# Ten batches of seven and eight key blocks a group in place of twelve of six, with the steps around them laid out anew

## The chip, the cores and the metric

The kernel runs on one core of a Trainium2 chip. The metric is the device time of one execution in microseconds (us). Engines are named as in the profile: PE (TensorE, matmuls), PEld (its weight loads), DVE (VectorE), ACT (ScalarE), POOL (GpSimd) and SP (SyncE, which here only issues DMAs).

## The reference

The input is a batch of four images of 384 channels and 48 x 48 = 2304 tokens, in float32. For each image:

- a depthwise 7 x 7 convolution with batch norm, then a layer norm over the channels: `local_q`;
- a layer norm of the image's tokens, then projections to queries, keys and values of eight heads of 48 channels;
- `q = q + local_q`, and attention of all 2304 tokens to all 2304 tokens in each head: `softmax(q k^T / sqrt(48)) v`;
- an output projection, a bias, and the image itself added.

```python
q = q + local_q
attn = jax.nn.softmax(jnp.einsum('bhnd,bhmd->bhnm', q, k) * scale, axis=-1)
out = jnp.einsum('bhnm,bhmd->bhnd', attn, v)
...
out = x_flat + (out @ proj_w.T + proj_b)
```

## The kernel before

**Tiling.** An image's queries are cut into five groups (8, 10, 10, 10 and 10 rows of 48 tokens, so 384 or 480 columns), which makes groups t = 0 to 19 over the four images; g = t mod 5. Heads are taken in four pairs p. The keys are 18 blocks of 128 tokens. So a group is 4 x 18 = 72 blocks, each a pair of heads against 128 keys.

**A block.** `score` (line 1105) multiplies the keys, in a high and a low part, with the queries, in a high and a low part: three steps, each a pair of matmuls on the two halves of the array's rows, into a PSUM buffer `r`. ScalarE takes the exponential into a tile `pt` (line 1113), of which there are four. `weigh` (line 1120) multiplies the values with `pt`, one head in each half of the array's columns, into a buffer `o`; the value's extra column of ones gives the softmax's denominator. All PSUM buffers, `r`, `o` and those of the projections, come from one pool of four, each of two banks, in turn.

**A batch.** `score_batch` issues the scores of six blocks, `weigh_batch` then weighs the six. A group has twelve such slots s, three to a pair of heads. ScalarE copies each batch's sum out of PSUM: the first of a pair to the output `ao` (line 1007; for the fourth pair to `aot`), the second and third to a tile `part_o` (line 997, two buffers), and VectorE adds it to the first in the next slot (`sums_add`, line 1016). After the last add of a pair SyncE stores the denominators (`den`, line 1021), and after the fourth pair it moves pieces of `aot` into `ao` (the tails, line 1025).

**Work between.** All engine queues are written out by hand, in the order of the loop over slots. VectorE's largest work is the convolution of later groups (line 340), one instruction a tap, handed out by `convolve` at two points in each slot; `plan` computes how many from an estimate of VectorE's spare time (`spare`) and from when each group's convolution is due. Around it stand:

- the next query: a norm in steps (`Norm`: sum, centre, squares on ScalarE at line 561, sum of squares, variance, root, then `local_end` and `query_end`). For groups up to 4 the means are matmuls (line 593), and VectorE waits for the root at line 631; later groups send partial sums through DRAM (`out`, then `few_in` at line 656);
- the norm of the next image's tokens, by the same steps, in an image's last groups;
- the split of each pair's queries: `high_queries` (a cast on ScalarE, line 968), `low_queries` (a subtraction on VectorE at line 973, then six DMAs on SyncE, lines 978 and 980). Pairs 1 to 3 are split in the first slot of the pair before. The fourth pair's queries are first gathered from the others' tails into `qt` (`gather_tails`, line 700, eight DMAs on SyncE), at s = 0;
- the previous group's division (`divide`, at s = 2): SyncE reads the denominators into `rd` (line 1032), VectorE takes reciprocals (line 1042), and SyncE spreads them; the product is taken at s = 7 (line 1446) and stored by POOL;
- the keys: a third of a pair's keys (six blocks, tile `ks`, three buffers) is loaded two slots ahead (`load_keys`, line 766), by POOL, and by ScalarE's queue at the start of an image.

Between images, keys and values of the next image are projected (line 694), with the output projection of the image before.

Of the kernel before, what the change touches and what calls it, by code (L numbers as in the profile page):

```python
# [25 lines left out]
BATCH = 6  # L26
NSLOT = 12
X_SLOTS = 4, 7
X_LATER = 3
OUT_SLOT = 7  # L30
# [18 lines left out]
def unshifted_pass(  # L49
# [120 lines left out]
    third = BATCH * P  # L170
# [257 lines left out]
    def norm_slots(t):  # L428
        return (8 - (t > 0), None) if t + 1 < NA else (5, 8)

    def spare(t, s, half):
        b, g = divmod(t, NA)
        first, second = norm_slots(t)
        time = 3.6 - (0.0 if half else 0.6) - (0.6 if half and s % 3 == 1 else 0.0)
        if b + 1 < B and g >= begins(b + 1):
            time -= {(2, 1): 2.3, (4, 1): 2.2, (5, 1): 2.3, (7, 0): 0.4, (8, 0): 2.6}.get(
                (s, half), 0.0
            )
        if g:
            time -= {(2, 0): 0.7, (7, 1): 1.4}.get((s, half), 0.0)  # L440
        if t + 1 < NA:
            if t:
                time -= {
                    (first, 0): 1.3,
                    (first + 1, 0): 1.4,
                    (first + 1, 1): 1.3,
                    (first + 2, 1): 4.3,
                    (first + 3, 1): 0.6,
                }.get((s, half), 0.0)
            else:  # L450
                time -= {(first + 1, 0): 1.4, (first + 2, 0): 4.3, (first + 2, 1): 0.6}.get(
                    (s, half), 0.0
                )
        elif g < NA - 1:
            time -= {
                (3, 1): 2.3, (5, 0): 1.2, (5, 1): 2.2, (6, 1): 2.3, (8, 0): 0.4, (8, 1): 1.5,
                (9, 0): 4.5,
            }.get((s, half), 0.0)
        return max(0.3, time) * columns_of(t) / G
# [21 lines left out]
    for t in range(NT):  # L481
        if t % NA == 0 and t:
            points += [("kv", t, g, h) for g in range(NG) for h in range(5)]
            room += [spare_at_keys(t // NA, g, h) for g in range(NG) for h in range(5)]
        points += [("slot", t, s, h) for s in range(NSLOT) for h in range(2)]
        room += [spare(t, s, h) for s in range(NSLOT) for h in range(2)]
# [4 lines left out]
    for t in range(1, NT):  # L491
        last = ("slot", t - 1, norm_slots(t - 1)[0] - (t >= NA), t < NA) if t % NA else ("kv", t, 4, 0)
# [203 lines left out]
    def gather_tails(dst, src):  # L696

        for i, c in enumerate((*range(CC), 0)):
            for r in (0, 64):
                nc.sync.dma_start(  # L700
                    out=dst[r + 16 * i : r + 16 * i + 16], in_=src[r + HD : r + 64, c, :]
                )
# [65 lines left out]
    def from_x(b, g, before=None, ao=None):  # L768
# [22 lines left out]
        def key(u, r):  # L791
# [7 lines left out]
            else:  # L799
                k = work.tile([P, 2, GM], HALF, tag="pt", name=f"k{b}_{g}_{u}", bufs=4)[:, :, :G]  # L800
# [143 lines left out]
    def query_end(t, at_once=False):  # L944
# [3 lines left out]
        q3 = work.tile([P, GM], F32, tag="qt", name=f"qt{t}", bufs=1)[:, : columns_of(t)]  # L948
        queries[t] = q, q3
# [36 lines left out]
    ended = []  # L986
    parts_of = deque()

    def sums_out():

        if not ended:
            return
        t, p, i, sums = ended.pop()
        n = columns_of(t)
        if i:
            part = work.tile([P, GM], F32, tag="part_o", name=f"o{t}_{p}_{i}")[:, :n]
            nc.scalar.copy(part[0 : 64 + HA], sums[0 : 64 + HA, 0, :n])  # L997
            parts_of.append((t, p, i, part))
            return
        if p == 0:  # L1000
            ao = work.tile([P, CC, GM], F32, tag="ao", name=f"ao{t}")[:, :, :n]
            ao3 = work.tile([P, GM], F32, tag="aot", name=f"aot{t}", bufs=1)[:, :n]
            den = dram.tile([NH, n], F32, tag=f"den{n}", name=f"den{t}")
            outputs[t] = ao, ao3, den
        ao, ao3, den = outputs[t]
        dst = ao[:, p, :] if p < CC else ao3
        nc.scalar.copy(dst[0 : 64 + HA], sums[0 : 64 + HA, 0, :n])  # L1007

    def sums_add():
# [3 lines left out]
        t, p, i, part = parts_of.popleft()  # L1013
        ao, ao3, den = outputs[t]
        dst = (ao[:, p, :] if p < CC else ao3)[0 : 64 + HA]
        nc.vector.tensor_add(dst, dst, part[0 : 64 + HA])  # L1016
        if i < KB // BATCH - 1:
            return
# [3 lines left out]
        if p == NP - 1:  # L1022
            for c in range(CC):
# [71 lines left out]
    jobs, between = deque(), deque()  # L1095
    weighing = deque()

    def score(t, p, kb):
        ks, qs = stacks[t // NA, p, kb // BATCH], stacked[t, p]
        at = slice(kb % BATCH * P, (kb % BATCH + 1) * P)  # L1100
# [11 lines left out]
        pt = work.tile([P, 2, GM], F32, tag="pt", name="pt", bufs=4)[:, :, :n]  # L1112
# [3 lines left out]
    def weigh(i, sums):  # L1116
        t, p, kb, pt = weighing.popleft()
        for j in range(2):
            first = (kb % NB * NH + 2 * p + j) * HA
            nc.tensor.matmul(  # L1120
                sums[halves[j], 0, : columns_of(t)],
                lhsT=values[t // NA, kb // NB][:, first : first + 64],
                rhs=pt[:, j, :],
                start=i == 0,
                stop=i == BATCH - 1,
            )

    def score_batch(t, s):
        p, k0 = s // (KB // BATCH), s % (KB // BATCH) * BATCH
        for kb in range(k0, k0 + BATCH):  # L1130
            score(t, p, kb)
            if between:
                between.popleft()()

    def weigh_batch(t, s):
        p, i = s // (KB // BATCH), s % (KB // BATCH)
# [4 lines left out]
        sums = two_banks("o")  # L1141
        for n in range(BATCH):
            weigh(n, sums)
        ended.append((t, p, i, sums))
        sums_out()
# [139 lines left out]

    for t in range(NT):
        b, g = divmod(t, NA)
        if g == 0 and b:

            sums_add()  # L1290
            load_x(b, NG - 1)
# [68 lines left out]
        first, second = norm_slots(t)  # L1360
        for s in range(NSLOT):
            pair, part = divmod(s, KB // BATCH)
            score_batch(t, s)
            if part == 0 and pair < NP - 1:
                high_queries(t, pair + 1)
            if s == 0:
                gather_tails(*reversed(queries[t]))
            if s == 0 and g == 0:
                keep_stack(b, 2)
            if (s or g) and (s < NSLOT - 2 or g < NA - 1):  # L1370
                load_keys(b, s + 2, nc.scalar if g == 0 and s < 3 else nc.gpsimd)
            if s == 2 and g:
                rb = divide(t - 1)
            if s == 0 and coming:
                load_x(b + 1, g - begins(b + 1))
            if s == NSLOT - 4 and g == NA - 1:
# [4 lines left out]
                else:  # L1381
                    places = [("acc", 3)] * 3 + [("sq", 2)] * 2 + [("qs", 5)]
                    aos = []
                    for i in range(NG):
                        load_residual(b, i, *places[i])
                        aos.append(fetch(b, i) if i < NG - 1 else outputs[t][0])
            if coming and s == X_SLOTS[1] + 1:
                norm_x.scale(norm_x.few_newton())
            if following and s == second + 1:
                local_end(t + 1, norm.few_newton())  # L1390
                query_end(t + 1, True)
            if coming and s == X_SLOTS[0] + 1:
                jobs.extend(norm_x.square_jobs())
            if following and s == first + 1:
                jobs.extend(norm.square_jobs())
            if coming and s == X_SLOTS[1]:
                norm_x.few_variance()
            if following and s == second:
                norm.few_variance()
# [3 lines left out]
            else:  # L1403
                convolve("slot", t, s, 0)
            sums_add()
# [8 lines left out]
            if coming and s == X_SLOTS[1]:  # L1414
                norm_x.few_root()
            if following and s == second:
                norm.few_root()
# [3 lines left out]
            weigh_batch(t, s)  # L1421
            if early and s == first:
# [5 lines left out]
            if early and s == first + (2 if t == 0 else 3):  # L1428
                low_queries(t + 1, 0)
            convolve("slot", t, s, 1)  # L1430
            if t and early and s == first + 2:
                local_end(t + 1, norm.newton())
                query_end(t + 1)
            if part == 0 and pair < NP - 1:
                low_queries(t, pair + 1)
            if t and early and s == first + 1:
                norm.sum_squares()
            if following and s == second + 1:
                low_queries(t + 1, 0)
            if coming and s == X_SLOTS[0]:  # L1440
                norm_x.few_centre()
            if following and s == first:
                norm.few_centre()
            if s == OUT_SLOT and g:
                ao = outputs[t - 1][0]
                nc.vector.tensor_mul(ao, ao, rb)
                hold(t - 1)
            if coming and s == X_SLOTS[0] - 2:
                norm_x = Norm(xn[b + 1, g - begins(b + 1)])
                norm_x.sum()  # L1450
                norm_x.out()
            if coming and s == X_SLOTS[0] + 1:
                norm_x.sum_squares()
                norm_x.out()
            if following and s == first - 2:
                norm = Norm(accs[t + 1])
                norm.sum()
                norm.out()
            if following and s == first + 1:
                norm.sum_squares()  # L1460
                norm.out()

    sums_add()
    for i, at in enumerate(pieces_out):
# [556 lines left out]
```

## Time and profile before

| | |
|---|---|
| Runs, us | 2743.88, 2743.94, 2736.79; median 2743.88 |
| The profiled execution's own time, us | 2739.04 |
| Its span, us | 2737.2 |
| Granted TensorE clock | 0.997 |
| PE / DVE / ACT busy, share of the span | 99% / 85% / 61% |
| Chain that ended last: PE o L1120, PE r L1105, PE r L694 | 42%, 34%, 13% |
| Score matmuls L1105, number and mean | 8640, 373 ns |
| Weighing matmuls L1120, number and mean | 5760, 554 ns |
| Exponentials L1113, number and mean | 1440, 943 ns |

A line of the timeline has start, duration, engine, line, operation, what it writes and reads with shapes, and how many instructions are merged in it; in brackets stands the idle time of the engine before it and what ended that. SPq is SyncE's queue of DMA issues. Matmuls overlap their neighbours, so the time of a run is read from its start to the start of the next, not from means. A weighing counts as two records in each half[...].

### The profile page before, as it was taken

Reading aid. Unit: us, or ns where it says so; the run is one execution under the profiler, and the core shown is the slowest. Engines: PE = TensorE matmul, PEld = TensorE weight load, DVE = VectorE, ACT = ScalarE, POOL = GpSimd, SP = SyncE. Lnnn points to the kernel's source line nnn. Section 1 sums busy time; section 2 is a strip of 40 time slices with the busy share of each in tenths; the row PEclk is TensorE's granted clock in tenths of the full one; section 3 lists DMA queues with packets and bytes.
Section 4 is the critical chain, followed back from the end, with each engine's and each line's share of the span. In section 5 each row is a group of like instructions: output and inputs, shape, how many; then the busy total and the mean of one; then the engine's idle time right before and its main releaser. Section 6 shows DMA issues by size and latency. Waiting matters only on the chain.

```text
span 2737.2 us, 46047 instructions
## 1 busy us (share of the span) xinstructions
PE 2714.7 (99%) x16438; PEld 1536.6 (56%) x16438; DVE 2314.8 (85%) x4038; ACT 1671.1 (61%) x2317; POOL 603.9 (22%) x1077
## 2 busy tenths in 40 slices
PE   8999999999999999999999999999999999999999
PEld 5565555555556555555555655555555565555555
DVE  7999999989999999989889999889888998986212
ACT  4356777777325777777622677777752377776762
POOL 5541101102453111011155211111225511110110
PEclk9999999999999999999999999999999999999999
DMA  8354544446465545354555553545635544444442
GB/s 164 85 143 136 142 115 129 124 136 182 101 160 154 139 120 146 115 152 124 143 140 138 166 147 110 142 126 141 152 105 158 147 140 133 139 132 132 139 150 68
DMA packets 160223, 370.46 MB, mean 135 GB/s; under 512 B 58672, under 2 KB 107472, under 8 KB 159984
## 3 DMA queue, kind: packets, MB, share of 16 engines
q0 software_dynamic: 71424, 279.04, 35.6%
q1 hardware_dynamic: 83248, 78.33, 12.6%
q10 hardware_dynamic: 5312, 10.06, 1.1%
q8 instruction: 132, 2.16, 0.3%
q14 instruction: 107, 0.88, 0.1%
HBM read 258.14 MB, written 64.14 MB: 118 GB/s over the span
## 4 chain that ended last, share of the span: by engine, by line
PE 90%; DVE 5%; DMA 4%; ACT 0%; issue 0%; SPq 0%; POOL 0%; DVEq 0%; POOLq 0%; ACTq 0%
PE o L1120 42%; PE r L1105 34%; PE r L694 13%; DVE acc L340 2%; DMA parts<-part 1%; DMA staged<-in_qkv_wT_dram 1%; DVE k L804 0%; DMA slab<-in_x_dram 0%; PE r L415 0%; DMA four<-parts 0%; DVE xn L689 0%; DMA wide<-k 0%; DMA xn<-in_x_dram 0%; DMA out_dram<-xr 0%; DVE xr L1086 0%
## 5 line engine op out<-in xcount | busy, mean ns | idle before, releaser
L340 DVE SCALAR_TENSOR_TENSOR acc<-slab,vec,acc 128x470 f32<-128x470 f32 (+10 forms) x2832 | 1658.1, 658 | 2.0 <-ACT acc L303 2.0
L1113 ACT ACTIVATE pt<-r 128x960 f32<-128x960 f32 (+1 forms) x1440 | 1248.6, 943 | 246.4 <-PE o L1120 151.8
L1120 PE MATMUL o<-pt,v 128*64 128x480 f32 (+1 forms) x5760 | 1166.2, 554 | 0.4 <-ACT pt L1113 0.4
L1105 PE MATMUL r<-qs,ks 64*128 64x480 f32 (+1 forms) x8640 | 967.0, 373 | 4.8 <-ACT xn L818 3.0
L1105 PEld LDWEIGHTS r<-qs,ks 64*128 64x128 f32 x8640 | 785.2, 184 | 268.2 <-issue 171.6
L1120 PEld LDWEIGHTS o<-pt,v 128*64 128x64 f32 x5760 | 392.5, 137 | 659.9 <-issue 566.5
L766 POOL DMA_DIRECT2D ks<-wide x220 | 160.0, 727 | 1369.7 <-PE r L1105 1310.0
L694 PE MATMUL r<-xn,w_qk 128*128 128x384 f32 x864 | 284.7, 487 | 0.0
L997 ACT COPY o<-o 113x480 f32<-113x480 f32 (+1 forms) x160 | 87.1, 544 | 277.3 <-PE o L1120 276.7
L694 PEld LDWEIGHTS r<-xn,w_qk 128*128 128x128 f32 x864 | 164.4, 191 | 115.3 <-issue 1.8
L694 PE MATMUL r<-w_v,xn 128*128 128x384 f32 x432 | 145.3, 489 | 2.8 <-DVE xn L689 1.4
L788 ACT COPY v<-r 128x384 f32<-128x384 f32 x72 | 32.0, 479 | 183.3 <-PE r L694 183.3
L1016 DVE TENSOR_TENSOR ao<-ao,o 113x480 f32<-113x480 f32 (+1 forms) x120 | 75.9, 633 | 73.9 <-ACT o L997 73.9
L694 PEld LDWEIGHTS r<-w_v,xn 128*128 128x128 f32 x432 | 81.1, 190 | 62.6 <-DVE xn L689 3.8
L973 DVE TENSOR_TENSOR qs<-xn,qs 128x480 fp32r<-128x480 f32 (+1 forms) x60 | 38.1, 635 | 63.8 <-ACT qs L968 63.8
L751 POOL DMA_DIRECT2D wide<-k x144 | 72.4, 505 | 78.3 <-ACT k L801 64.2
L694 PE MATMUL r<-af,w_o 128*128 128x384 f32 (+1 forms) x270 | 85.2, 470 | 0.0
L1007 ACT COPY ao<-o 113x480 f32<-113x480 f32 (+1 forms) x60 | 32.6, 544 | 72.1 <-PE o L1120 72.1
L1016 DVE TENSOR_TENSOR aot<-aot,o 113x480 f32<-113x480 f32 (+1 forms) x40 | 25.4, 634 | 56.9 <-ACT o L997 56.9
L818 ACT ACTIVATE xn<-r,qkb 128x384 f32<-128x384 f32 x72 | 39.6, 576 | 50.8 <-PE r L694 47.6
L1086 DVE SCALAR_TENSOR_TENSOR xr<-r,pb,xr 128x384 f32<-128x384 f32 (+2 forms) x72 | 42.0, 611 | 33.2 <-PE r L694 26.0
L694 PEld LDWEIGHTS r<-af,w_o 128*128 128x128 f32 x270 | 51.3, 190 | 31.9
(148 smaller groups left out, 1354.9 us busy)
## 6 DMA issues: line engine op xcount, KB each, us to landing
ks<-wide POOLq DMA_DIRECT2D x220, 768.0 KB, 4.9
qs<-qs SPq DMA_DIRECT2D x352, 60.0 KB
slab<-in_x_dram POOLq DMA_DIRECT2D x24, 432.0 KB, 7.2
wide<-k POOLq DMA_DIRECT2D x96, 96.0 KB, 2.2
wide<-ks POOLq DMA_DIRECT2D x12, 768.0 KB, 5.3
xr<-in_x_dram POOLq DMA_DIRECT2D x16, 576.0 KB, 5.6
rb<-rden SPq DMA_DIRECT2D x32, 270.0 KB
held<-ao POOLq DMA_DIRECT2D x12, 720.0 KB, 3.9
```

The lines of the kernel that those rows point to most:

```text
L340: nc.vector.scalar_tensor_tensor(dst, src, weight, dst, ALU.mult, ALU.add)
L694: nc.tensor.matmul(dst, lhsT=weights(c), rhs=src(c), start=c == 0, stop=c == CC - 1)
L751: nc.gpsimd.dma_start(out=last[16 * u : 16 * u + 16, 0], in_=k[r : r + 16, 0])
L766: queue.dma_start(out=place_keys(b, p, i), in_=wide[b, p][:, :, at])
L818: nc.scalar.activation(src[:, i, :], q[:, :G], AF.Identity, bias=qkb[:, 0, i : i + 1])
L973: nc.vector.tensor_sub(qs[:, 1, :], query_of(t, p), qs[:, 0, :])
L997: nc.scalar.copy(part[0 : 64 + HA], sums[0 : 64 + HA, 0, :n])
L1016: nc.vector.tensor_add(dst, dst, part[0 : 64 + HA])
L1086: nc.vector.scalar_tensor_tensor(xr[:, co, :], m, pb[:, co : co + 1], xr[:, co, :], ALU.add, ALU.add)
L1105: nc.tensor.matmul(r[:, j, :n], lhsT=ks[rows, w, at], rhs=qs[rows, m, :], start=i == 0, stop=i == 2,)
L1113: nc.scalar.activation(pt, r[:, :, :n], AF.Exp, scale=SCALE)
L1120: nc.tensor.matmul(sums[halves[j], 0, : columns_of(t)], lhsT=values[t // NA, kb // NB][:, first : first + 64], rhs=pt[:, j, :], start=i == ...
```

## The change

Groups 4 to 19 (`few_slots`: t + 1 >= 5) get ten slots of 7, 7, 7, 7, 8, 7, 7, 7, 7 and 8 blocks; groups 0 to 3 keep twelve of six. Slots 2 and 7 of ten hold the end of one pair and the start of the next (`crosses`): the weighing then fills two buffers `o`, each copied out by itself, and the pending add is taken ahead of the slot's convolution. So a group still has 12 copied sums and 8 adds.

Buffers: `pt` has five tiles instead of four; `part_o` has one instead of two; `aot` loses its own tile and takes the single buffer of `qt`. For that, `tails_out` (the six copies of tails) and `gather_tails` become steps of their own, in this order: in slot 0 ahead of the weighing in groups of twelve slots, in slot 2 in groups of ten.

The norm steps, the division and the product are placed by two tables, PLACES_12 and PLACES_10, as (slot, stage), where stage 0 is ahead of the slot's first convolution, 1 ahead of the weighing, 2 after it and 3 after the second convolution. PLACES_12 keeps the places of before, but for tails. In groups of ten, centring and squares stand in the same slot and stage, the division's reciprocal at (1, 1), the product at (5, 1), the high split of pairs 1 to 3 in slots 0, 2 and 4, and the first high split of the next group's queries between exponentials (`in_gap`). The plan's estimates and due times follow the slots. Key loads are issued after the slot in which a third ends, all by POOL in groups of ten.

```diff
+THIRD = 6
+PLACES_12 = {
+    "x_sum": (2, 3), "x_centre": (4, 3), "x_squares": (5, 0), "x_sum_squares": (5, 3),
+    "x_variance": (7, 0), "x_root": (7, 1), "x_scale": (8, 0),
+    "divide": (2, 0), "tails": (0, 1), "multiply": (7, 3), "fetch": (8, 0),
+}
+PLACES_10 = {
+    "x_sum": (1, 3), "x_centre": (3, 1), "x_squares": (3, 1), "x_sum_squares": (3, 3),
+    "x_variance": (5, 1), "x_root": (5, 1), "x_scale": (5, 3),
+    "divide": (1, 1), "tails": (2, 1), "multiply": (5, 1), "fetch": (7, 0),
+    "q_sum": (2, 3), "q_centre": (4, 1), "q_squares": (4, 1), "q_sum_squares": (4, 3),
+    "q_variance": (6, 1), "q_root": (6, 1), "q_end": (6, 3), "q_high": (6, 3), "q_low": (7, 3),
+}
+BATCHES = {12: [6] * 12, 10: [7, 7, 7, 7, 8] * 2}
+HIGHS = {12: (0, 3, 6), 10: (0, 2, 4)}
...
+    def gather_tails(t):
+
+        src = queries[t][0]
+        dst = work.tile([P, GM], F32, tag="qt", name=f"qt{t}", bufs=1)[:, : columns_of(t)]
+        queries[t] = src, dst
...
+        if ao3 is None:
+            outputs[t][1] = work.tile([P, GM], F32, tag="qt", name=f"aot{t}", bufs=1)[:, :n]
+        return outputs[t][1]
+
+    def sums_out(t, p, first, last, sums):
+
+        n = columns_of(t)
+        if first:
+            dst = partial(t, p)
+        else:
+            dst = work.tile([P, GM], F32, tag="part_o", name=f"o{t}_{p}", bufs=1)[:, :n]
+            parts_of.append((t, p, last, dst))
+        nc.scalar.copy(dst[0 : 64 + HA], sums[0 : 64 + HA, :n])
...
-        pt = work.tile([P, 2, GM], F32, tag="pt", name="pt", bufs=4)[:, :, :n]
+        pt = work.tile([P, 2, GM], F32, tag="pt", name="pt", bufs=5)[:, :, :n]
...
     def score_batch(t, s):
-        p, k0 = s // (KB // BATCH), s % (KB // BATCH) * BATCH
-        for kb in range(k0, k0 + BATCH):
-            score(t, p, kb)
+        start, n = batch(t, s)
+        for i in range(n):
+            score(t, *divmod(start + i, KB))
             if between:
                 between.popleft()()
+            while i == 4 and in_gap:
+                in_gap.popleft()()
...
-        sums = two_banks("o")
-        for n in range(BATCH):
-            weigh(n, sums)
-        ended.append((t, p, i, sums))
-        sums_out()
+        while i < end:
+            p, first = divmod(i, KB)
+            many = min(KB - first, end - i)
+            sums = two_banks("o")[:, 0]
+            for k in range(many):
+                weigh(k == 0, k == many - 1, sums)
+            sums_out(t, p, first == 0, first + many == KB, sums)
+            i += many
...
+            if here("tails"):
+                tails_out()
+                gather_tails(t)
...
-            if s == 0:
-                gather_tails(*reversed(queries[t]))
...
-            if (s or g) and (s < NSLOT - 2 or g < NA - 1):
-                load_keys(b, s + 2, nc.scalar if g == 0 and s < 3 else nc.gpsimd)
...
+            if few_slots(t):
+                start, n = batch(t, s)
+                if t == NA - 1 and s == 0:
+                    load_keys(b, 2)
+                for i in range(start // THIRD, (start + n) // THIRD):
+                    if i + 3 < NP * 3 or g < NA - 1:
+                        load_keys(b, i + 3)
+            else:
+                if s or g:
+                    load_keys(b, s + 2, nc.scalar if g == 0 and s < 3 else nc.gpsimd)
...
+            steps()
+            if n_slots(t) == 10 and crosses(t, s):
+                sums_add()
```

## The prediction

> **What bounds the kernel now.** I read the page's busy times first, then its chain of waits, then one batch in the timeline, engine by engine.
>
> ```profile
> PE 2714.7 (99%) x16438; PEld 1536.6 (56%) x16438; DVE 2314.8 (85%) x4038; ACT 1671.1 (61%) x2317; POOL 603.9 (22%) x1077
> ...
> PE 90%; DVE 5%; DMA 4%; ACT 0%; issue 0%; SPq 0%; POOL 0%; DVEq 0%; POOLq 0%; ACTq 0%
> ```
>
> TensorE is never idle for long, so only what shortens or interrupts its own row counts. The timeline of TensorE alone, one batch of group 6:
>
> ```profile
> 1003.76 4.17 PE L1105 MATMUL r<-qs,ks 64*128 64x480 f32 x36
> 1007.86 5.05 PE L1120 MATMUL o<-pt,v 128*64 128x480 f32 x24
> 1012.84 0.92 PE L1105 MATMUL r<-qs,ks 64*128 64x480 f32 x6
> ```
>
> The columns are start and duration. A batch takes 12.84 - 3.76 = 9.08 us: 4.10 for scores, 4.98 for weighing. By single instructions, pairs of score matmuls start 0.217 us apart and pairs of weighing matmuls 0.4025 us apart. A block is three of the first and two of the second: 3 x 0.2167 + 2 x 0.4025 = 1.455 us. Six blocks are 8.73; the other 0.35 us is the batch's own. It sits where the run changes kind: 0.31 us to the first weighing and 0.50 us back to the first score, and the first step of each run is longer (0.32 and 0.45). Nearly all 192 batches of groups 4 to 19 take this time to 0.03 us, so TensorE hardly ever waits there. Group 6 as a whole is 108.9 us with 103.9 us of VectorE work, so VectorE has little room.
>
> **What the Trainium skill says.** "TensorEngine Tiling (Array Packing)", Key Properties: "Mode switching requires drain". Scores use half the rows, weighing half the columns, so each batch switches twice; the trace agrees, with the gaps above. "TensorE: Matmul & The Clock Gate", Architectural detail, has ScalarE and VectorE strictly in order; the trace agrees (below, VectorE's sum stands behind a reciprocal that waits). "PSUM — Partial Sum Buffer", Specifications, gives eight banks; four buffers of two take all of them, so a score may need its predecessor's exponential. The trace shows this once: in group 0 a score began at 245.88, 0.05 us after an exponential's end at 245.83.
>
> **The change, part by part.**
>
> 1. *Fewer batches.* Groups 4 to 19 go from 12 to 10 batches with the same 72 blocks: 16 x 2 x 0.35 = **-11.1 us**. A batch with two pairs of heads adds no switch: its second sum continues the weighing run. Sums copied and added per group stay 12 and 8.
>
> 2. *Eight-block batches* (two a group). The sum's buffer is the one that the score four places back held, so the weighing waits for the fifth exponential. ScalarE in the same batch:
>
> ```profile
> 1003.88 0.56 ACT L997 COPY o<-o 113x480 f32<-113x480 f32 x1 [2.13 <-PE o L1120]
> 1004.78 3.56 ACT L1113 ACTIVATE pt<-r 128x960 f32<-128x960 f32 x4 [0.34 <-PE r L1105]
> 1008.99 1.83 ACT L1113 ACTIVATE pt<-r 128x960 f32<-128x960 f32 x2 [0.66 <-PE o L1120]
> ```
>
> The fifth now waits for the first weighing (0.66 us, for a weight buffer); the added `pt` buffer takes that wait away. The first ends 1.99 us after the batch's start and each next 0.86 later: the fifth at 5.43, plus 0.05. The scores would be done at 4.10 + 2 x 0.65 = 5.40. So 0.09 us is lost, in the 384-column groups by the same sum 0.15: 26 x 0.09 + 6 x 0.15 = **+3.2 us**. Seven blocks need the fourth (4.57 + 0.05 against 4.75): nothing lost. The ends are 0 (a drain overlaps the wait) and 6.
>
> 3. *SyncE's queue in groups 1 to 3.* These keep 12 batches, but the output's tails now share the buffer of the query tails, so the eight gathers are issued after the six tail copies, and wait until those have landed. In the order of the built program they stand ahead of the second pair's query pieces and of the read of the denominators (`rd`). Now:
>
> ```profile
> 255.83 5.01 SPq L700 DMA_DIRECT2D qt<-xn  x8
> 266.46 0.51 SPq L1021 DMA_DIRECT2D den<-aot  x2
> 267.01 3.67 SPq L1025 DMA_DIRECT2D ao<-aot  x6
> 271.98 0.51 SPq L978 DMA_DIRECT2D qs<-qs  x1
> ...
> 275.69 0.59 SPq L1032 DMA_DIRECT2D rd<-den  x1
> ```
>
> The eight took 5.01 us in an idle stretch; they move to 271.8 (the tails' last packet), and `rd` moves 5.2 us. What waits for it, on VectorE:
>
> ```profile
> 281.18 0.30 DVE L1042 RECIPROCAL rd<-rd 128x24 f32<-128x24 f32 x1 [1.34 <-DMA rd<-den]
> 281.51 0.40 DVE L1046 SCALAR_TENSOR_TENSOR inside<-rd,inside 128x24 f32<-128x24 f32 x2
> 281.83 3.08 DVE L340 SCALAR_TENSOR_TENSOR acc<-slab,vec,acc 128x450 f32<-128x450 f32 x5
> 284.82 0.65 DVE L1016 TENSOR_TENSOR ao<-ao,o 113x480 f32<-113x480 f32 x1
> ```
>
> Group 1 waited already, so it waits 2.7 to 5.2 us more (the low end if `rd` escapes the key load that it now meets); group 2 had 1 us in hand, group 3 none. The add at 284.82 stands 6.8 us after its batch's start (278.01); in groups 2 and 3 it stands at 7.5 and 6.7. The new plan puts about 0.6 us more convolution ahead of it, so I put these adds at 10.1 to 12.6, 12.3 to 14.3 and 10.8 to 12.5. The *partial-sum buffer goes from two to one*: the next copy of a sum, due 9.19 us after the batch's start, waits for that add. ScalarE's slack before TensorE feels it is 0.34 (idle before the first exponential) plus 0.34 (the third exponential, at 3.71, against the weighing at 4.10), so an add (0.65 long) later than 9.16 is paid in full: 0.9 to 3.4, 3.1 to 5.1, 1.6 to 3.3, together **+8.5 us** (5.6 to 11.8; 0 if the delay is absorbed before the add; a later transfer cannot gain). It doesn't run on: later in each of these groups VectorE waits for ScalarE, 5.24 us in group 1 (line 631), and that takes it up. The query pieces, 5 us later too, had 9 us.
>
> 4. *Steps laid out anew.* From group 4 on the reciprocal comes half a batch earlier, so VectorE waits for `rd` there: it landed 8 to 13 us after the low-query subtraction that precedes it, and 4 us of convolution stand between, so about 7 us a group instead of 1. Mostly this eats idle time: VectorE now waits up to 4 us for a copy at several adds of groups 8 to 17. But the centring now stands in the batch whose ScalarE queue squares its result. Behind the add come 2.3 us of centring and 1.9 of squares, then the batch's copy: an add later than about 7.7 us (6.9 for 384 columns) holds the copy, the exponentials, then TensorE. From the built order and measured durations I get adds at 8 to 10 us in groups 4, 6 and 7 and under 7 in all others: **+2.5 us** (0 to 6; a step put closer to its consumer cannot gain). One part buffer here bites only past 10.3 us.
>
> 5. *Costed at nothing.* Key loads: free at the end of a third's scores, needed 12 blocks (18 us) later, landing in 4.9; only a POOL queue blocked over 13 us would show. In groups 5, 10 and 15 two loads go from ScalarE's queue to POOL's, behind the key store at 848.17, needed at about 861.8. Tails and gathers from group 4 on, 11 us of SyncE: due two batches on. High queries cast between exponentials: 0.59 us under weighing that leaves ScalarE 2.9 us. The second pair's pieces of later groups keep 2 us or more in hand. All but the last rest on VectorE's lead. The projections between images stay; stalls of 1.4 and 1.9 us in the first and third may move by 2 us either way.
>
> Sum: -11.1 + 3.2 + 8.5 + 2.5 = +3.1. The profiled execution took 2739.04 us (span 2737.20); it would take 2742.1. The median of the runs is 2743.88, 4.8 above that, so I predict 2747.0.
>
> **Rivals.** *The cover holds (faster):* `rd` lands in time or the lag is absorbed before line 1016, and no square waits: -11.1 + 3.2 = -7.9, 2736; with no eight-block loss and quieter projections 2732. For it: in group 6 an add stood 9.7 us behind its batch's start without a stall. Against: two part buffers covered that one.
> *ScalarE held by squares (slower):* batches 3 and 4 of a group, deciding from an add at 7.7 us. If VectorE lies 2 us further back than I put it in the 12 groups that prepare the next query there, each loses about 1.5 us, 18 in place of my 2.5: 2762; in half of them, 2753. For it: VectorE has 5 us to spare in a group and takes 6 more of waits. Against: its idle time at the adds of groups 8 to 17.
> *That the switches aren't saved* is excluded by the built order: runs of 42 and 48 score matmuls.
>
> **How the numbers follow.** My case has 0.45 (2740 to 2753, of it 0.05 over the bound), the faster rival 0.28 (0.18 over the bound), the slower 0.27. About 0.3%, 8.2 us, is what a measurement of this kernel can tell from no change: faster 0.18, same 0.50, slower 0.32. The range reaches from the faster rival to the slower one's middle, 2733 to 2758; my case alone is 2740 to 2753.
>
> **What would show it.** Right: batches of 10.5 and 12.1 us at 480 columns, score-to-weighing runs of 4.75 and 5.49; in groups 1 to 3, one long score run in the fourth batch, ScalarE's copy waiting for VectorE's add, and a longer wait of the reciprocal. Wrong: groups 1 to 3 as long as before (step 3 fails), eight-block score runs of 5.40 (step 2), or stalls in batches 3 and 4 of groups 9 to 18 (the slower rival).

## The result, and the profile after

The changed kernel takes 2780.4 us (median of 6 runs, 2773.8 to 2789.5) against 2739.0 for the kernel before: a ratio of 1.0147, 95% interval 1.0127 to 1.0167. It is 41 us slower, well outside the predicted range of 2733 to 2758. The prediction started from the median of three runs, 2743.88; the median of all six is 2738.96. So against the forecast change of +3.1 us stands a measured one of +41.4.

The page of the profiled execution (2782.1 us, span 2780.3), its busy times and its chain of waits:

```profile
PE 2724.7 (98%) x16438; PEld 1546.1 (56%) x16438; DVE 2314.3 (83%) x4038; ACT 1660.0 (60%) x2317; POOL 605.5 (22%) x1083
...
PE 77%; DVE 12%; DMA 6%; SPq 2%; ACT 1%; issue 1%; ACTq 0%; POOL 0%; DVEq 0%
```

TensorE's share of the chain fell from 90 to 77%; VectorE, DMAs and SyncE's queue took it over. VectorE did the same work (2314 us), so something made it wait.

Where nothing waits, the change does what it says. TensorE in group 17, a batch of seven blocks and one of eight, each up to the start of the next (start, duration):

```profile
2414.47 4.81 PE L1150 MATMUL r<-qs,ks 64*128 64x480 f32 x42
2419.22 5.86 PE L1165 MATMUL o<-pt,v 128*64 128x480 f32 x28
2425.00 4.83 PE L1150 MATMUL r<-qs,ks 64*128 64x480 f32 x42
...
2456.62 5.54 PE L1150 MATMUL r<-qs,ks 64*128 64x480 f32 x48
2462.12 6.66 PE L1165 MATMUL o<-pt,v 128*64 128x480 f32 x32
2468.71 1.56 PE L1150 MATMUL r<-qs,ks 64*128 64x480 f32 x12
```

25.00 - 14.47 = 10.53 us for seven blocks, 68.71 - 56.62 = 12.09 for eight; their score runs last 4.75 and 5.50. These are the numbers that the prediction gave for "right".

The loss is in few places. I took each batch's time from the starts of its TensorE runs and subtracted what a batch of n blocks costs in the profile before (n x 1.455 + 0.35 us at 480 columns, n x 1.172 + 0.35 at 384). What is left over is its stall. Summed, and set against the same sums of the profile before (spans 2780.3 - 2737.2 = +43.1):

| | us |
|---|---|
| own time of 32 batches fewer, 0.346 each | -11.1 |
| eight-block batches, 26 at 0.10 and 6 at 0.17 | +3.6 |
| groups 7, 8 and 13, nearly all in the sixth batch (11.5, 11.3, 11.1, less the line above) | +33.3 |
| groups 2 and 3, fourth batch (6.05, 5.36) | +11.4 |
| group 6, fifth batch | +0.9 |
| first projection between images (148.55 against 140.92) | +7.6 |
| third projection (139.52 against 141.37) | -1.9 |
| groups 0 and 1; start and end | +0.8; -2.2 |

That is +42.4; the other 0.7 is spread. Twelve of the sixteen changed groups, all from 9 to 19 but 13 among them, run as forecast.

**The stall of group 8, followed back.** TensorE, then ScalarE, VectorE, SyncE's queue and GpSimd's, in timelines of one engine each (brackets: idle before, and what ended it):

```profile
1231.92 2.22 PE L1150 MATMUL r<-qs,ks 64*128 64x480 f32 x18
1242.23 5.17 PE L1150 MATMUL r<-qs,ks 64*128 64x480 f32 x24 [8.08 <-ACT o L1047]
```

```profile
1240.14 1.59 ACT L597 ACTIVATE sq<-acc 128x480 f32<-128x480 f32 x3 [10.51 <-DVE acc L700]
1241.64 0.54 ACT L1047 COPY o<-o 113x480 f32<-113x480 f32 x1
```

```profile
1222.25 0.66 DVE L1056 TENSOR_TENSOR ao<-ao,o 113x480 f32<-113x480 f32 x1
1237.45 0.25 DVE L692 TENSOR_REDUCE few<-four 128x15 f32<-128x60 f32 x1 [14.54 <-DMA four<-parts]
1237.73 0.68 DVE L699 STREAM_TRANSPOSE sq<-few 128x480 f32<-128x480 f32 x1
1238.45 1.66 DVE L700 SCALAR_TENSOR_TENSOR acc<-sq,acc 128x1440 f32<-128x1440 f32 x1
```

```profile
1204.17 4.37 SPq L1070 DMA_DIRECT2D ao<-aot  x6
1218.31 5.19 SPq L739 DMA_DIRECT2D qt<-xn  x8
1223.60 1.20 SPq L1016 DMA_DIRECT2D qs<-qs  x1
...
1228.06 0.58 SPq L682 DMA_DIRECT2D parts<-part  x1
1235.13 0.59 SPq L683 DMA_DIRECT2D four<-parts  x1
```

```profile
1205.57 2.19 POOL L125 DMA_DIRECT2D slab<-in_x_dram  x4 [2.91 <-DVE acc L351]
```

Read from the TensorE lines on: TensorE has three blocks scored and waits; ScalarE's copy and exponentials stand behind three squares; the squares wait for VectorE's centring (line 700); that waits 14.5 us for the next query's sums, which go through DRAM (`parts`, then `four`). The sums were ready at 1210.3 (end of the reduction at line 679), but SyncE issued them only at 1228.06. Ahead of them stood the gathers, and the gathers had waited 9.6 us for the tail copies to land, since both now use the tile `qt`. In the middle of the tails GpSimd issued its load of the next slab, the part of the image that the convolution reads: two pieces of 432 KB and two of 144 KB, 1.2 MB (the expectations below say 0.9). That this load made the tails slow is shown by the run no_slab.

In the kernel before, the same exchange of group 8 went out 1.2 us after its sums, and VectorE waited 1.9 us. The gathers of that group came at its end, at 1243.89. VectorE, then SyncE's queue:

```profile
1186.45 0.65 DVE L643 TENSOR_REDUCE part<-sq 128x15 f32<-128x480 f32 x1
...
1199.42 0.25 DVE L656 TENSOR_REDUCE few<-four 128x15 f32<-128x60 f32 x1 [1.89 <-DMA four<-parts]
```

```profile
1188.30 0.59 SPq L646 DMA_DIRECT2D parts<-part  x1
1194.91 0.60 SPq L647 DMA_DIRECT2D four<-parts  x1
```

The way through DRAM has two legs, and the second is issued when the first has landed. The first took 6.6 us before and 7.1 us after, so a long leg is not new; what is new is that it starts 17.8 us after the sums. In no_slab it took 2.6 us. In the changed kernel it met other loads: GpSimd's queue was held as well, its row loads for the next image waited 13.3 us (the release is booked to SyncE's query pieces), and two key loads of 768 KB behind them went out together with `parts`:

```profile
1226.45 1.63 POOL L125 DMA_DIRECT2D xn<-in_x_dram  x3 [13.30 <-DMA qs<-qs]
1228.09 1.47 POOL L805 DMA_DIRECT2D ks<-wide  x2
```

That these key loads lengthened the leg is read from the timeline; no run moved them by themselves.

The Trainium skill, "DMA: Bandwidth & Descriptors", section "Issuing engines are not separate DMA queues", says that DMAs of all issuing engines run on the same 16 DMA engines and interleave. The trace agrees: in groups 8 and 13, where a slab load on GpSimd's queue fell among SyncE's tails, the first gather was issued 9.8 and 9.0 us after the last tail's issue had ended; in all other groups it was 1.4 to 4.5 us. "Perfetto Trace Analysis", DMA Instruction — HWDGE (DVE, Sync), adds that an issue's duration leaves out the data movement; here too, the six tails show 4.37 us and had landed only 14 us after the first was issued. I had priced these steps by such durations.

### The profile page after: what moved, and what is told of

The parts are those of the page before. It is cut to its first block, busy times and chain, and to the rows that moved or that the text cites. A ratio compares the mean times of both kernels' runs of the same rounds, so it can differ in the third digit from the quotient of the medians.

```text
span 2780.3 us, 45929 instructions
## 1 busy us (share of the span) xinstructions
PE 2724.7 (98%) x16438; PEld 1546.1 (56%) x16438; DVE 2314.3 (83%) x4038; ACT 1660.0 (60%) x2317; POOL 605.5 (22%) x1083
## 4 chain that ended last, share of the span: by engine, by line
PE 77%; DVE 12%; DMA 6%; SPq 2%; ACT 1%; issue 1%; ACTq 0%; POOL 0%; DVEq 0%
PE o L1165 34%; PE r L1150 28%; PE r L730 15%; DVE acc L351 8%; DMA parts<-part 2%; DMA four<-parts 1%; DMA ao<-aot 1%; SPq L1018 1%; DMA rd<-den 1%; DMA staged<-in_qkv_wT_dram 1%; DMA wide<-k 0%; SPq L1070 0%; DVE k L843 0%; DMA xn<-in_x_dram 0%; ACT pt L1158 0%
## 5 line engine op out<-in xcount | busy, mean ns | idle before, releaser
L125 POOL DMA_DIRECT2D xn<-in_x_dram x72 | 39.7, 554 | 174.8 <-DVE qs L1011 103.4
L692 DVE TENSOR_REDUCE few<-four 128x12 f32<-128x48 f32 (+1 forms) x66 | 15.6, 237 | 67.6 <-DMA four<-parts 67.5
```

What stands on the lines that cost most here:

```text
L125: queue.dma_start(out=dst[p0 : p0 + piece.shape[0]], in_=piece)
```

## The experiments

All are edits of the changed kernel, with times as a ratio to the kernel before and its 95% interval. Theory A: SyncE's order in groups of ten batches. Theory B: the layout of norm steps is too tight in itself. Theory C, added later: the meeting of transfers. Stalls per group are from each run's profile.

**exchange_first: the exchange ahead of tails and gathers**

```diff
-    "divide": (1, 1), "tails": (2, 1), "multiply": (5, 1), "fetch": (7, 0),
+    "divide": (1, 1), "tails": (3, 0), "multiply": (5, 1), "fetch": (7, 0),
```

> One place is moved, (3, 0) for (2, 1) under "tails" in the ten-batch table, so that on SyncE the exchange of the next queries' sums (lines 682 and 683) stands ahead of the six tail copies and the eight gathers; VectorE, ScalarE and TensorE keep their order. Theory A (the loss of groups 7, 8 and 13 is SyncE's order: the gathers wait for tails that land late beside slab loads, and the exchange waits behind them): the stalls of 11.5, 11.3 and 11.1 us in these groups go, VectorE's wait for four<-parts falls from 67 to some 35 us, and the time to about 2748. Groups 2 and 3 and the first projection between images keep their stalls. If the gathers now land after 53 us of a group, up to 3 us a group come back. Theory B (the new layout of the norm steps is too tight for ScalarE and VectorE in themselves, whatever SyncE does): no change, 2778 to 2783.

Measured: 2775.6 us, 1.0148 (1.0120 to 1.0176). VectorE's wait for `four<-parts` fell from 67.5 to 29.5 us (33.2 in the kernel before), and groups 8 and 13 from 11 to 1.7 and 0.5, as A has it. But seven groups, 8 among them, now had stalls of 1.5 to 5.5 us in that sixth batch. ScalarE in group 7:

```profile
1119.81 0.59 ACT L1006 CAST qs<-qt 128x480 fp32r<-128x480 f32 x1 [5.39 <-DMA den<-ao]
1120.31 1.58 ACT L597 ACTIVATE sq<-acc 128x480 f32<-128x480 f32 x3
```

The cast of the query tails now waits (the release is booked to another DMA), since the last gather of this group was issued at 55.1 us, past the cast's own place at 52. The caution in the expectation, put at up to 3 us a group, took back what the order gave, so 2748 was missed by 28 us. So both ends of the queue are tight: neither side can be served first as long as gathers follow tails at once.

**tails_early: only the tails leave**

```diff
-    "divide": (1, 1), "tails": (2, 1), "multiply": (5, 1), "fetch": (7, 0),
+    "divide": (1, 1), "tails": (1, 1), "gather": (2, 1), "multiply": (5, 1), "fetch": (7, 0),
...
             if here("tails"):
                 tails_out()
+            if here("gather"):
                 gather_tails(t)
```

> In the ten-batch groups the tail copies alone go from (2, 1) to (1, 1), behind the read of the denominators and ahead of the exchange for the next image; the gathers stay at (2, 1), still ahead of the exchange of the next queries' sums. Theory A with the landing as its cause: the tails have a batch to land in, the gathers no longer wait 10 us for them, the exchange is then only the 9 us of issues later that it also is in groups 16 to 18, which run without a stall: stalls of groups 7, 8 and 13 go, about 2748. If instead the 14 issues ahead of the exchange are enough to make it late, with no waiting for a landing, half or more of the 33 us stays: 2765 to 2780. Theory B: no change.

Measured: 2753.3, 1.0057 (1.0042 to 1.0072): 27 us back. Groups 8 and 13 stall by 0.2 and 0.5. Group 7 keeps 6.5: there the gathers' issue still delays the exchange, which is then issued among rows of the next image and two key loads, and its second leg takes 6.3 us. In this profile group 3 hardly stalled (0.4), so the whole gain is not the tails'. The landing was the larger part of the cause, not the issues. The norm steps stand where they stood, so theory B does not explain these stalls.

**gather_alone: only the gathers leave**

```diff
-    "divide": (1, 1), "tails": (2, 1), "multiply": (5, 1), "fetch": (7, 0),
+    "divide": (1, 1), "tails": (2, 1), "gather": (3, 0), "multiply": (5, 1), "fetch": (7, 0),
```

> One step of the ten-batch groups moves: the eight gathers go from (2, 1) to (3, 0), behind the exchange of the next queries' sums; the tail copies stay at (2, 1). It is the run exchange_first with the tails left where they were, so a batch passes between tails and gathers. If what hurts is that the exchange stands behind gathers that wait for a landing: the stalls of groups 7, 8 and 13 go (-33), and as the tails have landed by then, the gathers are not late for the cast either: some 2747, with groups 2 and 3 and the projection as in the kernel after. If the tails' issue ahead of the exchange suffices to make it late: 2760 to 2775.

Measured: 2752.9, 1.0047 (1.0030 to 1.0063), with the step split as in tails_early. Groups 7, 8 and 13: 2.3, 0.6, 0.4. The exchange was not behind the gathers, and VectorE's wait fell to 30.1 us. Group 4 got 4.1, and groups 2 and 3 kept 5.6 and 5.0. Tails ahead of the exchange cost little; gathers that wait ahead of it cost 9 to 11 us in each of these three groups.

**no_slab: the other transfer taken away**

```diff
+        if b:
+            slabs[b, g] = (slabs[0, 3][0], first, end)
+            return
```

> The kernel after, but the slabs of images 2 to 4 (the windows that the convolution reads, 0.6 to 0.9 MB a group) are not loaded: the convolution of those images reads a slab of the first image that stays in place. Everything else, SyncE's order and all arithmetic, stays. Theory C (a slab load that meets the tail copies or an exchange is what makes them late): groups 8 and 13, where the load was issued in the middle of the tail copies, lose their 11 us, and the first projection between images goes from 148 to some 141; group 7, where its load was already over and its own exchange and the next image's rows were in the way, may keep its stall: together 22 to 41 us less, 2740 to 2758. Rival (the tails' own copies and the key loads are slow enough): groups 8 and 13 keep theirs, 2770 or more.

Measured: 2750.2, 1.0053 (1.0036 to 1.0070). SyncE's queue is that of the changed kernel. Group 8 again:

```profile
1189.22 4.43 SPq L1073 DMA_DIRECT2D ao<-aot  x6
1195.35 5.71 SPq L742 DMA_DIRECT2D qt<-xn  x8
...
1204.97 0.59 SPq L685 DMA_DIRECT2D parts<-part  x1
1207.58 0.58 SPq L686 DMA_DIRECT2D four<-parts  x1
```

The gathers follow the tails by 1.7 us instead of 9.8, the exchange goes out 15.8 us after the first tail instead of 23.9. Groups 8 and 13 stall by 0.2 each, the first projection takes 141.35 us, and group 7 keeps 9.5: its tails start late (33.2 us into the group, behind the next image's own exchange) and meet that image's rows, which were still loaded; the second leg of its exchange, issued just after two key loads, takes 6.4 us. All three as theory C said. So the stalls of groups 8 and 13 needed both: the new order, and a load that meets it. For group 7 the order is shown by gather_alone; which loads it met is read from the timeline only.

**slab_late: the same load, later**

```diff
-            load_slab(*divmod(t + 1, NA))
+            if t < NA:
+                load_slab(*divmod(t + 1, NA))
+            else:
+                slab_due.append(t + 1)
...
+            if t >= NA and g == 0 and s == 0 or t >= NA - 2 and s == n_slots(t) - 3:
+                slab_out()
```

> SyncE's queue stays as in the kernel after; what moves is the load of the next slab of the image (line 125, 0.9 MB, on GpSimd's queue): from group 3 on it is asked for in the eighth batch (ninth or tenth of twelve), or at the start of an image's first group, where no statistics are exchanged, instead of where the convolution before it ends (batch 2 or 3, and the fifth step of the projections). Theory C (the cause is the meeting of this load with small transfers that others wait for; SyncE's order alone would fit): the gathers of groups 7, 8 and 13 no longer wait 10 us for the tail copies, these stalls fall from 11 to under 2 us a group, and the first projection between images goes from 148 back to some 141 us: together about -40, 2740. Theory A in the form that the order on SyncE is the cause and the load only one delay among many: stalls move to other groups, 2760 to 2780.

Measured: 2775.2, 1.0147 (1.0121 to 1.0173), no gain that can be told from the changed kernel's 1.0147, where 40 us were expected, because the load did not move where it mattered. GpSimd's queue alone is not written out by hand (what was said of all queues holds for the other four); its order is found when the program is built, and in group 8 the load stood where it had stood:

```profile
1203.95 2.21 POOL L125 DMA_DIRECT2D slab<-in_x_dram  x4 [2.91 <-DVE acc L363]
```

Groups 7, 8 and 13 kept 11.0, 7.3 and 8.3. In the first projection it did move, and that fell from 148.55 to 141.07, but a stall of 3.9 us came at the start of group 5 and one of 2.2 in group 6. In the changed kernel, GpSimd's queue, SyncE's and VectorE there:

```profile
808.11 2.20 POOL L125 DMA_DIRECT2D slab<-in_x_dram  x4
```

```profile
807.02 0.58 SPq L682 DMA_DIRECT2D parts<-part  x1
809.63 0.59 SPq L683 DMA_DIRECT2D four<-parts  x1
```

```profile
819.22 0.23 DVE L692 TENSOR_REDUCE few<-four 128x12 f32<-128x48 f32 x1 [7.07 <-DMA four<-parts]
```

The second leg of an exchange, issued 1.5 us after the first of four slab pieces, landed 9.6 us later and kept VectorE waiting 7.1 us. Where the load went later the loss went; where it stayed, most of the loss stayed.

**squares_later: the carrier moved**

```diff
-    "q_centre": (4, 1), "q_squares": (4, 1), "q_sum_squares": (4, 3),
+    "q_centre": (4, 1), "q_squares": (5, 0), "q_sum_squares": (5, 3),
```

> The squares of the next queries go from (4, 1), the batch of their centring, to (5, 0), so that ScalarE meets them behind the next batch's exponentials; their sum goes from (4, 3) to (5, 3). SyncE's queue keeps its order up to there. Theory A with ScalarE as the carrier: VectorE waits as long as before for four<-parts in groups 7, 8 and 13 (10 to 15 us each), but nothing that TensorE needs stands behind the squares any longer: the stalls fall from 11 to 0 to 3 us a group, 2745 to 2757. If VectorE's own lateness (the add) is what carries the delay to TensorE: no gain, 2778 to 2783. The exchange of the sum of squares, a batch later, may cost up to 2 us a group at the variance.

Measured: 2796.6, 1.0214 (1.0196 to 1.0232): 16 us worse, which neither expectation had. In groups 7, 8 and 13 the sixth batch's stall fell (10.0, 11.0, 10.7 to 2.6, 4.4, 0), but the next two batches got up to 6.0, and groups 9 and 12 stalled by 6.0 and 7.7. VectorE's wait for `four<-parts`, in the view of that tile:

```profile
  DMA four<-parts: 114.9, 30
```

It was 67.5 us, 21 times. The sum of squares, a batch later, became the next exchange to be late. So squares carried the delay to ScalarE, but moving them doesn't cure it. How much of the stall is due to the carrier alone stays open.

**gather_late_12: groups of twelve batches**

```diff
-    "divide": (2, 0), "tails": (0, 1), "multiply": (7, 3), "fetch": (8, 0),
+    "divide": (2, 0), "tails": (0, 1), "gather": (2, 1), "multiply": (7, 3), "fetch": (8, 0),
```

> Only the twelve-batch groups 0 to 3 change: the eight gathers go from (0, 1), where they stand between the tail copies and the read of the denominators, to (2, 1), behind that read and the copies that follow it. Step 3 of the prediction (the read is pushed back by the gathers, the reciprocal holds VectorE, the add is late, and with one part buffer ScalarE's next copy waits for it): the stalls of 6.1 and 5.3 us in groups 2 and 3 go, about 2769. Rival, that these stalls come from the single part buffer or from the new convolution plan alone: 2778 to 2783. The stalls of groups 7, 8 and 13 stay in both.

Measured: 2772.4, 1.0120 (1.0103 to 1.0137), again with the step split. The fourth batches of groups 2 and 3: 0.0 and 0.0; the others kept theirs, and group 12 had one too this time (9.6). Group 2 of the changed kernel, SyncE, VectorE, ScalarE:

```profile
384.22 4.93 SPq L739 DMA_DIRECT2D qt<-xn  x8
...
393.59 0.58 SPq L1077 DMA_DIRECT2D rd<-den  x1
```

```profile
398.12 0.34 DVE L1087 RECIPROCAL rd<-rd 128x30 f32<-128x30 f32 x1 [6.39 <-DMA rd<-den]
...
401.82 0.65 DVE L1056 TENSOR_TENSOR ao<-ao,o 113x480 f32<-113x480 f32 x1
```

```profile
402.56 0.56 ACT L1047 COPY o<-o 113x480 f32<-113x480 f32 x1 [8.13 <-DVE ao L1056]
```

and VectorE with the gathers moved:

```profile
392.60 0.34 DVE L1087 RECIPROCAL rd<-rd 128x30 f32<-128x30 f32 x1
...
396.30 0.65 DVE L1056 TENSOR_TENSOR ao<-ao,o 113x480 f32<-113x480 f32 x1
```

The group began at 370.0 and 370.9, so the add stands 6.5 us earlier in it (25.4 instead of 31.9), the reciprocal doesn't wait, and the part buffer, of which there is still one, costs nothing. It only hands a late add on.

**best1, best2, best3, best4: put together.** best1 has tails at (1, 1), gathers at (3, 0), and (2, 1) in groups of twelve; best2 tails at (0, 1); best3 is best1 with slab_late; best4 moves the gathers of an image's first group to (1, 1) and its slab to the second batch.

> Three places: in ten-batch groups the tail copies at (1, 1) and the gathers at (3, 0), behind the exchange of the next queries' sums; in twelve-batch groups the gathers at (2, 1), as in the run gather_late_12. If the two losses are independent, this adds what both runs gained: groups 2 and 3 without stalls (-6.3 on the run tails_early), group 7 without its remaining 6.5, so about 2740. If the cast of the query tails (line 1006 on ScalarE, 53 us into a group) now comes ahead of the gathers' landing, as in the run exchange_first, 2 to 5 us a group in several groups come back: 2750 to 2765. The first projection between images keeps its 145 to 148 us.

> As best1, with the tail copies of ten-batch groups at (0, 1), right behind the add that completes them, as in the kernel before. They then stand ahead of the read of the denominators: in groups 4 to 7, where the add is late, that read comes up to 4 us later and VectorE's reciprocal with it. If VectorE's lead covers that, as it did in the kernel before: about 2738 to 2742, like best1. If not, 1 to 4 us a group in groups 4, 6, 7 more than best1.

> best1 and slab_late together. If the meeting of transfers is the cause of what best1 leaves (the first projection between images, single stalls at the fifth and sixth batch): the saving of step 1 less step 2 appears, 2738 - 7 = 2731, with kv at 140 to 142 us. If the slab in the eighth batch collides with the next queries' pieces or the key loads instead, stalls of 1 to 5 us appear in batches 8 and 9 or at a group's start: 2738 to 2750.

> best3 with two places changed: the first group of an image, which has no tail copies ahead of its gathers, issues them at (1, 1), so that they are in time for the cast of the query tails; and the slab of an image's first group is asked for in the second batch, not the first. If the stalls that best3 kept there are of these causes (0.8 us in group 10's sixth batch, 1.8 us at the start of group 5): 2734 to 2736, a ratio of 0.998 to 1.000. If the slab's pieces are spread between the key stores anyway, group 5 keeps its stall: 2736 to 2738.

Measured: best1 2742.5, 1.0012 (1.0006 to 1.0019); best2 2742.8, 1.0014 (1.0008 to 1.0021); best3 2736.8, 0.9997 (0.9987 to 1.0006); best4 2736.6, 0.9998 (0.9990 to 1.0007). The gains add nearly as expected for best1 (2740); best3 is 6 us above its expectation of 2731. Where the tails stand among the early batches doesn't matter (best2). With the slab's move the first projection fell from 147.06 to 140.36 us (best3). best4's profile has group 10's stall gone (1.3 to 0.5, of which the eight-block batches are 0.3), but keeps 1.7 at the start of group 5, the second case of its expectation. Its chain of waits:

```profile
PE 92%; DVE 5%; DMA 2%; issue 0%; ACT 0%; SPq 0%; DVEq 0%; ACTq 0%; POOL 0%
```

TensorE is back on it. No version beats the kernel before by what can be measured: of the 11.1 us saved, 3.6 go to eight-block batches, and stalls of about 1 us each in groups 0, 6 and 7 and 1.7 in group 5 take more of it.

**nine: nine batches of eight**

```diff
-BATCHES = {12: [6] * 12, 10: [7, 7, 7, 7, 8] * 2}
+BATCHES = {12: [6] * 12, 9: [8] * 9}
```

> best4 with nine batches of 8 in groups 4 to 19 instead of ten of 7, 7, 7, 7 and 8; the places of the steps keep their batch numbers. Steps 1 and 2 of the prediction by themselves: one switch less a group saves 0.35 us, seven more eight-block batches cost 0.10 each at 480 columns and 0.17 at 384 (as the trace of the kernel after shows for its two): +0.35 in 12 groups and +0.84 in 4, together +7.6 on best4, about 2743. If eight-block batches back to back leave ScalarE no time to catch up (8 exponentials of 0.86, a copy of 0.56 and steps of up to 3 us in 12.1), stalls of 1 us or more at single batches come on top: 2750 to 2765. If they cost nothing of their own (the fifth exponential is early): -5.6, 2730.

Measured: 2757.3, 1.0069 (1.0052 to 1.0085), 21 us above best4. Groups 16 to 18 show the steady part: 1.4 us a group, about 0.1 in each of nine batches and 0.5 more in the third, where a pair ends after two blocks and the second sum waits:

```profile
2307.34 1.83 PE L1177 MATMUL o<-pt,v 128*64 128x480 f32 x8
2309.50 3.04 PE L1177 MATMUL o<-pt,v 128*64 128x480 f32 x14 [0.33 <-ACT pt L1170]
```

That 0.5 was in no expectation. On top came single stalls (6.5 in group 11, 2.1 in group 6) at a first batch, within the second expectation's numbers; their cause was not followed up. The price of an eight-block batch is confirmed; more of them don't pay.

## Why the prediction was wrong

1. *Fewer batches, -11.1.* Right: batches of 10.53 and 12.09 us. (As written, 16 x 2 x 0.35 is 11.2; the 11.1 follows from 0.346.)
2. *Eight-block batches, +3.2.* Right: 0.10 and 0.17 each instead of 0.09 and 0.15, +3.6.
3. *SyncE's queue in groups 1 to 3, +8.5 (5.6 to 11.8).* Right in mechanism, shown by gather_late_12; the sum was 0.19 + 6.05 + 5.36 = 11.6. Group 1 was put too high: its read landed in 1.9 us and its add stood at 9.13, just under the bound of 9.16. Groups 2 and 3 were put too low. Their adds stood 13.7 and 13.2 us after the batch's start; by my bound that costs 4.5 and 4.0, but 6.05 and 5.36 were paid. The term that was off is ScalarE's slack: of the two times 0.34 us that I took off the delay, only 0.1 to 0.2 was to be had (the copy came 5.2 and 4.7 us late, the score runs grew by 5.0 and 4.6), and the weighing of the same batch lost another 0.8 to 1.0. The landing is the rest of the spread: in the profile of tails_early, group 3's read landed 2.0 us after its issue instead of 4.6, and the group lost 0.4.
4. *Steps laid out anew, +2.5.* About right in size: 0.9 and 1.3 in the fifth batch of groups 6 and 7, none in group 4. No run tested whether late adds are their cause.
5. *Costed at nothing: failed.* The step that cost some 32 us, the 33.3 of the table less group 7's 1.3 above, is "Tails and gathers from group 4 on, 11 us of SyncE: due two batches on". I asked when they themselves were due, and not who stood behind them. The exchange of the next query's sums did, and its deadline is the centring two batches on. In step 3 I had followed the same queue past `rd`, group by group, but not past this exchange, and from group 4 on I gave the wait for the tails' landing no price at all. GpSimd's queue reached the 13 us that I named for the key loads (13.3 in group 8); TensorE did not wait for these keys, but they met the exchange. The projections, put at 2 us either way, moved by 7.6 in the first by the same kind of meeting: a slab load came to lie among the transfers of an exchange. The run no_slab shows the load's part in groups 8 and 13 and in the projection; tails_early and gather_alone show the order's part in groups 8 and 13, gather_alone also in group 7. That the gathers wait for the tails at all follows from the program, in which both use `qt`; no run gave `aot` a tile of its own again.

The slower rival named the right place, ScalarE held by squares in that batch, and the wrong cause. It priced VectorE's own lateness at 1.5 us in each of up to 12 groups; what came was one late exchange, 10 to 11 us in three groups. The sign that I gave for it, "stalls in batches 3 and 4 of groups 9 to 18", did not show: the stalls are in batch 5, counted from 0, and of those groups only in 13. The faster rival's 2736 is near what best3 and best4 measured, but only by chance: it was a saving of 7.9 us from 2743.88, and these two save 0.6 and 1.5 us by the medians against the kernel before, measured beside them (2737.3 and 2738.2), with intervals that include no change.

## What to carry to other kernels

When an issue is moved on a queue that runs in order, list everything behind it up to its new place, with the deadline of each, and price the wait that goes with it, not the issue's duration. Where two tiles share a buffer, look at what lies between the transfer that frees it and the one that fills it; here a batch between them took 27 of the 41 us away (tails_early, gather_alone), while the exchange put ahead of both gained nothing (exchange_first). Give a transfer through DRAM that an engine waits for slack for the loads that can meet it; here one leg of an exchange took 9.6 us beside a slab load, where quiet ones took about 2.

## What the runs showed that I had not expected

- The delay depends on which transfers happen to meet, so a single profile gives a sample: group 12 stalled by 9.6 us in one profile and by 0.2 in another with the same order of steps in groups of ten, and group 3 by 5.4 and 0.4.
- The same read of the denominators, 0.6 us of issue, landed in 1.8 to 5.0 us where VectorE waited for it, within one profile.
